# A branch in place of VectorE's bound on a softplus, expert blocks skipped by row count, and a reordered end, in a fused selective-scan, attention and expert kernel

## The chip, the cores and the metric

The kernel runs on one core of a Trainium2 chip. The metric is the device time of one execution in microseconds (us). The engines are called as the profile calls them: PE is TensorE's matmul and PEld its weight load, DVE is VectorE, ACT is ScalarE, POOL is GpSimd, SP is SyncE, which here issues most DMAs. All data are fp32.

## The reference

Four images of 384 channels and 32x32 pixels (L = 1024 tokens) pass two layers.

```
x = x + gelu(LN(cross_merge(selective_scan(cross_scan(group_norm(x))))))   # layer 0
#   four directions k, 16 states n, for each channel d along the 1024 tokens:
#   dt = softplus(w_dt . dts + bias);  h = h*exp(dt*A) + dt*u*B;  y = sum_n h*C
t = tokens(x)
t = t + causal_attention(LN(t))                                            # layer 1
t = t + sum_e gate_e * (gelu(LN(t) w1_e + b1_e) w2_e + b2_e)               # top 2 of 4 experts
```

## The kernel before

**The scan sets the clock.** The layer-0 work is cut into 768 units (4 images, 3 channel blocks, 4 directions, 4 groups of states, 4 groups of channels; 192 units an image). One Python loop of ticks t writes the program; nothing reorders it afterwards, and each engine runs its own instructions in the order in which they were written. In tick t ACT gets the decay of unit t+2 (`decay`, an Exp, tile da), DVE the product `front` (tile v, a PSUM tile, L648) and the scan `middle` (tile h, L654), POOL the product `back` of unit t-1 (h times C, L671), which waits until `front` of tick t is over, and every fourth tick PE gets `row` (L696), 16 matmuls that sum four h tiles into y. There are seven h buffers. In images 1 to 3, `ahead` puts a wait on DVE before `front` in every fourth tick: for the row that was written two ticks earlier. In image 0, 104 units get v from PE instead (L958).

**Beside the scan.** A generator `preparation(b)` makes the inputs of image b while image b-1 is scanned. Its part `project_dt` runs for each direction k and channel block m (48 times; the first two, at the very start, in `first_dt`): PE projects, ACT adds the bias, then the softplus:

```
for x_, log in zip(xs, logs): act(log, x_, AF.Exp)
for log in logs:              act(log, log, AF.Ln, bias=1.0)
nc.vector.scalar_tensor_tensor(x_, log, BOUND, x_, ALU.min, ALU.max)   # L485, BOUND = 80
```

and DVE multiplies by u (L526). Both results go to HBM and come back spread over the partitions.

**Layer 1 behind it.** When an image's scan is over, `finish` (layernorm, gelu, residual), then `behind` (attention, the routing `ready`, the experts) are stepped while the next image is scanned; for the last image they stand alone, which the code calls `alone`. In each tick `go_on` gives such work a budget of PE time: `pace`, 4.4 in attention and 3.1 in the experts; each piece of work says what it costs. The experts of an image take 11 blocks of 256 token rows (NBLK), sorted by expert; block j has twelve parts (six of the first matmul, `first_`, L1591, six of the second, `second_`, L1636) that are charged 2.6 each, and its tokens' transposes 0.9. The order is first(0), first(1), second(0), first(2), second(1), and so on. Weights come by SP in 384 KB pieces (L1497) into eight slots. `by_rows` runs a block with fewer columns, or not at all, from a table of row counts, but only for the last image: PE loads all 11 counts (L1558) and branches (L1561, L1564). There each PSUM bank is first zeroed by DVE (L1584, L1627).

**The end.** `ready` is run for token groups of 4, 2 and 2 blocks of 128: gate scores, softmax over four experts, the comparison that picks two (`cnt`, `sel`), running sums and PE's prefix sums (`place`), the target rows (`places`, L1370), then 16 scatters by POOL (L1385) into the expert order. `combine` gathers each token's two results (POOL, L1682), adds residual, bias and gates on PE (L1708) and writes out (ACT, L1715). For the last image it is split in `early` (first choice, residual, bias) and `late` (second choice).

Of the kernel before, what the change touches and what calls it, by code (L numbers as in the profile page):

```python
# [47 lines left out]
PACE_E = 3.1  # L48
BT = 256
BOUND = 80.0  # L50
# [5 lines left out]
def hybrid_kernel(  # L56
# [419 lines left out]
    def softplus(xs, logs):  # L476

        for x_, log in zip(xs, logs):
            act(log, x_, AF.Exp)
        for log in logs:  # L480
            act(log, log, AF.Ln, bias=1.0)

    def bounded(x_, log):

        nc.vector.scalar_tensor_tensor(x_, log, BOUND, x_, ALU.min, ALU.max)  # L485

    def project_dt(b, pair, m, u, xd):

        both = PAIRS[pair]
        groups = (both,) if b == 0 else ((both[0],), (both[1],))  # L490
        v = u[m]
        for n, ks in enumerate(groups):
            need = 2 * len(ks) + (pair if n == 0 else 0)
            slots.kept = need
            while not slots.ready(need):
                yield "wait", 1
            slots.kept = 0
            if pair == 1 and n == 0:
                v = slots.now(f"ut_{b}_{m}", P, L)
                nc.scalar.copy(v.rearrange("p (w h) -> p w h", h=HW), columns(u[m]))  # L500
            dts = [slots.now(f"dt_{b}_{k}_{m}", P, L) for k in ks]
            dus = [slots.now(f"du_{b}_{k}_{m}", P, L) for k in ks]
            for h in range(NH):
                while not banks.ready(len(ks)):
                    yield "wait", 1
                pss = [banks.now(f"pdt_{b}_{k}_{m}_{h}") for k in ks]
                for i, k in enumerate(ks):
                    o = 64 * pair + 32 * both.index(k)
                    r = slice(o, o + R)
                    nc.tensor.matmul(  # L510
                        pss[i], wdt[r, m * P : (m + 1) * P], xd[r, bass.ts(h, 512)],
                        start=True, stop=True,
                    )
                if h == 0 or clock[0] >= IMAGE:

                    yield "wait", 1
                for i, k in enumerate(ks):
                    act(
                        dts[i][:, bass.ts(h, 512)], pss[i], AF.Identity, bias=dtb[:, k, m : m + 1]
                    )  # L520
                    banks.give(f"pdt_{b}_{k}_{m}_{h}")
            softplus(dts, dus)
            yield "wait", 2
            for i, k in enumerate(ks):
                bounded(dts[i], dus[i])
                nc.vector.tensor_mul(dus[i], dts[i], v)  # L526
                yield "wait", 1
                nc.sync.dma_start(dts_d[b, k][0, m * P : (m + 1) * P, :], dts[i])
                nc.sync.dma_start(dts_d[b, k][1, m * P : (m + 1) * P, :], dus[i])
                if b == 0:  # L530
                    stored_du.add((k, m))
                slots.give(f"dt_{b}_{k}_{m}", f"du_{b}_{k}_{m}")
        if pair == 1:
            slots.give(f"ut_{b}_{m}")
# [4 lines left out]
    def first_dt(u, xd):  # L539
# [13 lines left out]
        softplus(dts, dus)  # L553
        for i, k in enumerate(ks):
            bounded(dts[i], dus[i])
# [664 lines left out]
    def ready(b, h, yb, rows, moments):  # L1220
# [59 lines left out]
        def over(v):  # L1280
# [3 lines left out]
        nc.vector.tensor_reduce(red, sc, AX.X, ALU.max)  # L1284
        nc.vector.tensor_tensor(sc, sc, over(red), ALU.subtract)
        act(sc, sc, AF.Exp)

        cmp = [
            one.tile([P, 4, E, E], F32, tag=f"cmp{i}", name=f"cmp{i}_{name}")[:, :n] for i in range(2)
        ]  # L1290
        each = sc.unsqueeze(3).to_broadcast([P, n, E, E])
        other = sc.unsqueeze(2).to_broadcast([P, n, E, E])
        yield "wait", 1
        nc.vector.tensor_reduce(red, sc, AX.X, ALU.add)
        nc.vector.reciprocal(red, red)
        nc.vector.tensor_tensor(sc, sc, over(red), ALU.mult)
        nc.vector.tensor_tensor(cmp[0], other, each, ALU.is_gt)
        nc.vector.tensor_tensor(cmp[1], other, each, ALU.is_ge)
        nc.vector.tensor_tensor(
            cmp[1], cmp[1], lower.unsqueeze(1).to_broadcast([P, n, E, E]), ALU.mult  # L1300
        )
        nc.vector.tensor_tensor(cmp[0], cmp[0], cmp[1], ALU.max)
        cnt = small("cnt", name, n, E)
        nc.vector.tensor_reduce(cnt, cmp[0], AX.X, ALU.add)

        sel = small("sel", name, E, n)
        nc.vector.tensor_single_scalar(sel.rearrange("p e q -> p q e"), cnt, 1.5, ALU.is_lt)
        cum = counts[b, h] = sm.tile([P, E, n], F32, tag=f"cum{h}", name=f"cum_{name}")
        nc.vector.tensor_tensor_scan(
            cum.rearrange("p e q -> p (e q)"), fresh[n].rearrange("p e q -> p (e q)"),  # L1310
            sel.rearrange("p e q -> p (e q)"), 0.0, op0=ALU.mult, op1=ALU.add,
        )
# [22 lines left out]
        if h == LAST:  # L1335
            for i in range(LAST + 1):
                nc.tensor.matmul(
                    pp[:, 4 * E : 5 * E], ones, last_of(i, False),
                    start=(i == 0), stop=(i == LAST),
                )  # L1340
        yield "pe", 1.5
        mk = small("mk", name, n, E)
        nc.vector.scalar_tensor_tensor(mk, cnt, 1.5, sc, ALU.is_lt, ALU.mult)
        nc.vector.tensor_reduce(red, mk, AX.X, ALU.add)
        nc.vector.tensor_scalar_add(red, red, 1e-9)
        nc.vector.reciprocal(red, red)
        nc.vector.tensor_tensor(mk, mk, over(red), ALU.mult)
# [25 lines left out]
        banks.give(f"place_{name}")  # L1373
        pm = yield from banks.take(f"pm_{name}")
# [7 lines left out]
        placed = places[b]  # L1382
        for q in range(n):
            for i in range(2):
                nc.gpsimd.indirect_dma_start(  # L1385
                    out=views[2 * (q0 + q) + i],
                    out_offset=bass.IndirectOffsetOnAxis(
                        ap=placed[:, q0 + q, i : i + 1], axis=0
                    ),
                    in_=rows[:, q, :], in_offset=None,  # L1390
                )
            if not alone and q < n - 1:
                yield "wait", 1
        routed.add((b, h))
# [16 lines left out]
    def table(b, total):  # L1411
# [6 lines left out]
        nc.vector.tensor_reduce(n, full, AX.X, ALU.add)  # L1418
        up_to = one.tile([1, E - 1, E], F32, tag="up_to", name=f"up_to_{b}")
# [38 lines left out]
    def experts(b, route):  # L1458
# [11 lines left out]
        def look_up(j):  # L1470
            if j not in expert:
# [79 lines left out]
        def by_rows(j, run):  # L1551

            if not alone:
                run(BT)
                return
            if not filled:
                for n in range(NBLK):
                    filled[n] = nc.tensor.value_load(  # L1558
                        tables[b][0:1, 2, n : n + 1], min_val=0, max_val=BT
                    )  # L1560
            with tc.If(filled[j] > P) as whole:  # L1561
                run(BT)
            with whole.Else():
                with tc.If(filled[j] > 0):  # L1564
                    run(P)

        STEP = 3 if alone else 1

        def first_(j):
# [4 lines left out]
            for f0 in range(0, NF, 2 * STEP):  # L1574
# [3 lines left out]
                for f in range(f0, f0 + 2 * STEP, 2):  # L1578
# [4 lines left out]
                    if alone:  # L1583
                        nc.vector.memset(ps, 0.0)  # L1584
# [11 lines left out]
                by_rows(j, run)  # L1596
# [12 lines left out]
                yield "pe", 2.6 * STEP  # L1609
# [8 lines left out]
        def second_(j, gone):  # L1618
            pss = {}
            for c0 in range(0, 6, STEP):  # L1620
                for c in range(c0, c0 + STEP):
                    yield from need(("2", j, c))
                if c0 == 0:
                    for i in range(2):
                        pss[i] = yield from banks.take(f"py_{b}_{j}_{i}")
                        if alone:
                            nc.vector.memset(pss[i][:, :C], 0.0)  # L1627
# [14 lines left out]
                by_rows(j, run)  # L1642
                slots.give(*[tiles["2", j, c][1] for c in range(c0, c0 + STEP)])
                yield "pe", 2.6 * STEP
            yt = yield from slots.take(f"yt_{b}_{j}", P, 2, C)

            def out_():
                for i in range(2):
                    if alone and i == 1:
# [6 lines left out]
                if alone and j == NBLK - 2:  # L1656
                    side.append(early(b))
# [4 lines left out]

        while (b, LAST) not in routed:
            yield "wait", 1
        yield from load(0)
        yield "wait", 1
        yield from turn_(0)
        gone = {}
        for w, j in order_:
            if w == "1":  # L1670
                if j + 1 < NBLK:
                    yield from load(j + 1)
                yield from first_(j)
# [75 lines left out]
    def early(b):  # L1749

        for i in range(L // P):
# [4 lines left out]
            closing[i] = g, z  # L1756
            gather(b, i, g, 0)
            beside(b, i, g, z)
        yield "wait", 3
        for i in range(L // P):  # L1760
            ps = yield from banks.take(f"pz_{b}_{i}")
            add_up(ps, *closing[i], ("t2", "b2", 0), True, False)
            closing[i] = *closing[i], ps
            yield "pe", 2.0

    def late(b):

        for i in range(L // P):
            gather(b, i, closing[i][0], 1)
        for i in range(L // P):  # L1770
            while len(closing[i]) < 3:
                yield "wait", 1
            g, z, ps = closing[i]
            add_up(ps, g, z, (1,), False, True)
            put_out(b, i, ps, z)
# [61 lines left out]
    def go_on():  # L1837
        spare[0] = min(spare[0] + pace[0], pace[0])
# [115 lines left out]
```

## Time and profile before

| | |
|---|---|
| Time, median of 3 runs | 3740.76 us (3736.13 to 3742.01) |
| The profiled execution | 3738.39 us, span 3736.7 us (1.7 us lie around the span) |
| PE, DVE, ACT, POOL busy | 80%, 81%, 55%, 53% |
| First and last scan (L654) start at | 48.9 and 3155.7 us |
| Last row of y written by PE | about 3164 us |
| First query projection of the last image (L1068) | 3228.42 us |
| First expert matmul of the last image (L1591) | 3377.11 us |
| Last real block copied out (L1652); last output copied (L1715) | 3688.56; 3733.03 us |

All durations and places are of the one profiled execution. A row of the groups reads: line, engine, operation, out<-in, count, then busy us, mean ns of one, and the idle time in front of it with what ended it. In the matmul groups one written fp32 matmul is two records.

### The profile page before, as it was taken

To read this page: it belongs to the slowest core of one execution; us is meant where nothing else is said; L and a number is where in the kernel's file an instruction comes from. 1 tells how busy PE (TensorE), PEld (TensorE's weight loads), DVE (VectorE), ACT (ScalarE), POOL (GpSimd) and SP (SyncE) were. 2 spreads that over 40 slices of the span, in tenths; PEclk is the share of its full clock that TensorE was granted. 3 is DMA by queue.
4 is the path that set the end of the run, shared out by engine and by line. 5 is a ranking of instruction groups with operands and counts; after the bars stand their busy time and mean duration, and the time that the engine had idled before them with its cause. 6 is when DMAs were issued, how large, how long until landed. Compare 5 with 4: busy or idle time off the path is not lost. (4 is left out here: it accounts for less than half of the span.)

```text
span 3736.7 us, 41646 instructions
## 1 busy us (share of the span) xinstructions
PE 2996.1 (80%) x13267; PEld 1798.4 (48%) x13267; DVE 3020.3 (81%) x2417; ACT 2061.5 (55%) x3268; POOL 1980.5 (53%) x931
## 2 busy tenths in 40 slices
PE   4566755678589899779569999779589999778997
PEld 1233423334346566344345665344256665556775
DVE  6999888899989999998999999999989998131110
ACT  5778787556466566456546665356356564342121
POOL 2677667645656555764656555765666666010001
PEclk7677777779789999769779999879689999888998
DMA  6658644543577888554567888553378876215555
GB/s 198 216 201 291 241 179 186 201 166 135 195 243 277 293 300 297 198 196 153 177 224 277 292 286 292 193 206 129 123 253 301 294 279 207 76 47 180 180 187 178
DMA packets 405202, 798.42 MB, mean 214 GB/s; under 512 B 47500, under 2 KB 278620, under 8 KB 404972
## 3 DMA queue, kind: packets, MB, share of 16 engines
q1 hardware_dynamic: 390572, 770.01, 59.3%
q0 software_dynamic: 8192, 25.17, 2.1%
q8 instruction: 117, 1.92, 0.2%
q10 hardware_dynamic: 6208, 0.39, 0.1%
q14 instruction: 113, 0.93, 0.1%
HBM read 680.44 MB, written 115.02 MB: 213 GB/s over the span
## 5 line engine op out<-in xcount | busy, mean ns | idle before, releaser
L671 POOL TENSOR_TENSOR h<-h,bc 128x1024 f32<-128x1024 f32 x768 | 1818.4, 2372 | 1208.9 <-DVE v L648 1031.8
L654 DVE TENSOR_TENSOR_SCAN h<-da,v 128x1024 f32<-128x1024 f32 x768 | 1749.3, 2283 | 80.7 <-PE v L958 40.8
L192 ACT ACTIVATE da<-dt,a 128x1024 f32<-128x1024 f32 x768 | 884.7, 1162 | 774.8 <-DVE h L654 636.7
L648 DVE TENSOR_TENSOR v<-du,bc 128x1024 f32<-128x1024 f32 x664 | 851.4, 1282 | 95.9 <-PE y L696 26.2
L696 PE MATMUL y<-h,sel 128*32 128x512 f32 x3072 | 560.0, 703 | 186.2 <-POOL h L671 178.6
L1591 PE MATMUL ph<-turned,w 128*128 128x256 f32 (+1 forms) x2772 | 631.1, 384 | 45.4 <-DMA w<-in_w 32.2
L1636 PE MATMUL py<-w,ht 128*128 128x384 f32 x1776 | 606.2, 493 | 11.3 <-DMA w<-in_w 11.3
L1591 PEld LDWEIGHTS ph<-turned,w 128*128 128x128 f32 x2772 | 523.4, 193 | 164.2 <-issue 51.1
L1636 PEld LDWEIGHTS py<-w,ht 128*128 128x128 f32 x1776 | 335.2, 192 | 277.7 <-issue 40.0
L192 ACT ACTIVATE ht<-ph,b1t 128x256 f32<-128x256 f32 x470 | 196.7, 471 | 330.6 <-PE ph L1591 329.8
L696 PEld LDWEIGHTS y<-h,sel 128*32 128x32 f32 x3072 | 104.4, 120 | 507.7 <-POOL h L671 290.6
L1682 POOL DMA_INDIRECT g<-ysd,places x64 | 83.4, 1303 | 369.6 <-DMA g<-gtd 329.8
L958 PE MATMUL v<-ident,st 128*128 128x128 f32 x832 | 156.5, 351 | 117.4 <-DVE h L654 113.0
L192 ACT ACTIVATE st<-turn,bt 128x128 f32<-128x128 f32 x832 | 245.4, 564 | 0.1
L958 PEld LDWEIGHTS v<-ident,st 128*128 128x128 f32 x832 | 127.7, 183 | 164.0 <-DVE h L654 94.6
L182 ACT ACT_TABLE_LOAD x122 | 156.5, 1283 | 12.2 <-issue 10.1
L510 PE MATMUL pdt<-xd,wdt 12*128 12x512 f32 x184 | 117.2, 774 | 23.5 <-ACT st L192 7.2
L1385 POOL DMA_INDIRECT xsd<-fx,places x32 | 36.3, 1135 | 153.6 <-DVE places L1370 145.8
L1169 PE MATMUL po<-vt,pt 128*128 128x384 f32 x242 | 91.6, 528 | 9.0 <-ACT pt L1059 9.0
L1098 PE MATMUL ss<-axn,qt 128*128 128x512 f32 (+3 forms) x252 | 91.8, 508 | 5.6 <-ACT pr L192 4.5
L192 ACT ACTIVATE dt<-pdt,dtb 128x512 f32<-128x512 f32 x96 | 64.6, 690 | 49.4 <-PE pdt L510 48.1
L192 ACT ACTIVATE ht<-ht 128x3072 f32<-128x3072 f32 x33 | 91.3, 2766 | 0.4
(381 smaller groups left out, 2656.1 us busy)
## 6 DMA issues: line engine op xcount, KB each, us to landing
w<-in_w SPq DMA_DIRECT2D x528, 384.0 KB
bc<-rows SPq DMA_DIRECT2D x384, 512.0 KB
dt<-dts SPq DMA_DIRECT2D x192, 512.0 KB
du<-dts SPq DMA_DIRECT2D x192, 512.0 KB
dts<-dt SPq DMA_DIRECT2D x48, 512.0 KB
dts<-du SPq DMA_DIRECT2D x48, 512.0 KB
xg<-xsd SPq DMA_DIRECT2D x44, 384.0 KB
ysd<-yt SPq DMA_DIRECT2D x44, 384.0 KB
```

The costliest lines, as they stand in the source:

```text
L182: nc.scalar.preload_act_table_set(kind)
L192: return nc.scalar.activation(dst, src, f, **more)
L510: nc.tensor.matmul(pss[i], wdt[r, m * P : (m + 1) * P], xd[r, bass.ts(h, 512)], start=True, stop=True,)
L648: return nc.vector.tensor_tensor(u["v"], spread["du4", n], spread["bc", n][:, 0, :], ALU.mult)
L654: nc.vector.tensor_tensor_scan(u["h"][:, ::step], u["da"][:, ::step], u["v"][:, ::step], 0.0, op0=ALU.mult, op1=ALU.add,)
L671: product = units[n]["product"] = nc.gpsimd.tensor_tensor(h, h, spread["bc", n][:, 1, :], ALU.mult)
L696: units[n]["row"] = nc.tensor.matmul(y, sel, h, start=first, stop=last, tile_position=(0, jj * DJ))
L958: nc.tensor.transpose(u["v"][:, t * P : (t + 1) * P], st[:, t, u["j"] * P : (u["j"] + 1) * P], ident)
L1098: nc.tensor.matmul(ps[:, : e - o], qt[:, c, i * P : (i + 1) * P], xn[o // 512][:, c, : e - o], start=(c == 0), stop=(c == M - 1 and (alone ...
L1169: nc.tensor.matmul(po[:, :C], pts[i][:, j, :], vt[:, j, :], start=False, stop=(j == i))
L1591: nc.tensor.matmul(ps[:, i * BT : i * BT + n], t[:, c, i * P : (i + 1) * P], xt[:, c, :n], start=(c == 0), stop=(c == M - 1),)
L1636: nc.tensor.matmul(pss[i][:, :C], hts[j][:, 2 * c + f, i * P : (i + 1) * P], tiles["2", j, c][0][:, f, :], start=(c == 0 and f == 0), stop ...
```

## The change

1. The softplus. Exp now also gives the sum over its row; PE adds the 128 sums, DVE compares the total with 1e19, POOL and ACT load the answer into a register and branch. The usual way has only the Ln; the other way (POOL and ACT) bounds the argument at 40. DVE's pass L485 is gone from `project_dt`; `first_dt` clips before Exp and takes a maximum after it.
2. `by_rows` holds for all images: PE loads one row count per block in images 0 to 2, branches at each part, and where rows are left out fills the rest of the PSUM bank with transposes. DVE's zeroing is gone. A part is charged 2.2 instead of 2.6.
3. Block 0 is taken as expert 0, so its weights need no table; in the last image four pieces of weights are asked for before the routing is over, and the counts are loaded ahead of the first transposes.
4. Last image: `ready` picks on the raw scores, does the softmax after PE's prefix sums, and scatters before the gates are normalised. Pace is 1.5 after the scan.
5. Last image: residual, gates and bias are fetched from block 2 on (`beside_all`), DVE adds the first choice to the residual (`first_choice`), PE sums up in `late`.

```diff
+PACE_T = 1.5
+PART = 2.2
-BOUND = 80.0
+LIMIT = 1.0e19
+EDGE = 40.0
...
+        sums = sm.tile([P, 2], F32, tag="sums", name=f"sums_{names[0]}")
+        for i, (x_, log) in enumerate(zip(xs, logs)):
+            act(log, x_, AF.Exp, accum_out=sums[:, i : i + 1])
+        return sums
+    def within(sums, n, name):
+        ps = yield from banks.take(f"sums_{name}")
+        nc.tensor.matmul(ps[:1, :n], ones[:, :1], sums[:, :n], start=True, stop=True)
+        yield "wait", 1
+        fits = sm.tile([1, 2], I32, tag="fits", name=f"fits_{name}")
+        nc.vector.tensor_single_scalar(fits[:, :n], ps[:1, :n], LIMIT, ALU.is_le)
+        banks.give(f"sums_{name}")
+        yield "wait", 1
+        return fits
+    def bounded(x_, log, fits):
+        tables_for(LOGS)
+        fit = nc.values_load(
+            fits, engines=[mybir.EngineType.Pool, mybir.EngineType.Activation],
+            min_val=0, max_val=1,
+        )
+        with tc.If(fit != 0) as fast:
             act(log, log, AF.Ln, bias=1.0)
-        nc.vector.scalar_tensor_tensor(x_, log, BOUND, x_, ALU.min, ALU.max)
+        with fast.Else():
+            nc.gpsimd.tensor_scalar_min(log, x_, EDGE)
+            act(log, log, AF.Exp)
+            act(log, log, AF.Ln, bias=1.0)
+            nc.gpsimd.tensor_scalar(x_, x_, -EDGE, 0.0, ALU.add, ALU.max)
+            nc.gpsimd.tensor_tensor(log, log, x_, ALU.add)
...
-            yield "wait", 2
+            yield "wait", 1
+            fits = yield from within(sums, len(ks), f"{b}_{ks[0]}_{m}")
             for i, k in enumerate(ks):
-                bounded(dts[i], dus[i])
-                nc.vector.tensor_mul(dus[i], dts[i], v)
+                bounded(dts[i], dus[i], fits[:, i : i + 1])
+            yield "wait", 1
+            for i, k in enumerate(ks):
+                nc.vector.tensor_mul(dts[i], dus[i], v)
...
-            if not alone:
-                run(BT)
-                return
...
             with tc.If(filled[j] > P) as whole:
                 run(BT)
             with whole.Else():
-                with tc.If(filled[j] > 0):
+                fill(P)
+                with tc.If(filled[j] > 0) as some:
                     run(P)
+                with some.Else():
+                    fill(0)
...
-                    if alone:
-                        nc.vector.memset(ps, 0.0)
...
+                def fill(o):
+                    for f, t, w, name, ps in parts:
+                        for i in range(2):
+                            nc.tensor.transpose(
+                                ps[:, i * BT + o : i * BT + o + P], ident, ident
+                            )
...
-                yield "pe", 2.6 * STEP
+                yield "pe", PART * STEP
...
+        while alone and fetched[0] < 4:
+            while not slots.ready():
+                yield "wait", 1
+            weights()
         while (b, LAST) not in routed:
             yield "wait", 1
         yield from load(0)
+        for j in range(NBLK if alone else 1):
+            count_rows(j)
...
+    def first_choice(b):
+        for i in range(L // P):
+            gather(b, i, closing[b, i][0], 0)
+        yield "wait", 2
+        for i in range(L // P):
+            add_choice(b, i, 0)
+            yield "wait", 0
     def late(b):
         for i in range(L // P):
-            gather(b, i, closing[i][0], 1)
+            gather(b, i, closing[b, i][0], 1)
+        pss = {}
         for i in range(L // P):
-            while len(closing[i]) < 3:
-                yield "wait", 1
-            g, z, ps = closing[i]
-            add_up(ps, g, z, (1,), False, True)
-            put_out(b, i, ps, z)
+            pss[i] = yield from banks.take(f"pz_{b}_{i}")
+            sum_up(b, i, pss[i], False)
...
     def go_on():
+        if clock[0] >= NU + 4:
+            pace[0] = PACE_T
```

## The prediction

> **What bounds the kernel now.** The page's slices first: DVE is full through the scan and nearly idle after it, and PE fills up once in each image. So there are two stages, a scan bounded by DVE and an end bounded by chains and PE.
>
> ```profile
> PE   4566755678589899779569999779589999778997
> DVE  6999888899989999998999999999989998131110
> ```
>
> The timeline inside the scan gives the rhythm. A tick is one L648 and one L654, 1.26 + 2.29 us with small gaps: 3.61 us from L648 to L648. POOL's product begins when L648 ends, is over near the end of the scan, and POOL then idles 1.26 us.
>
> ```profile
> 3143.49 1.25 DVE L648 TENSOR_TENSOR v<-du,bc 128x1024 f32<-128x1024 f32 x1
> 3144.78 2.29 DVE L654 TENSOR_TENSOR_SCAN h<-da,v 128x1024 f32<-128x1024 f32 x1
> 3144.91 2.36 POOL L671 TENSOR_TENSOR h<-h,bc 128x1024 f32<-128x1024 f32 x1 [1.26 <-DVE v L648]
> 3147.10 1.26 DVE L648 TENSOR_TENSOR v<-du,bc 128x1024 f32<-128x1024 f32 x1
> ```
>
> The groups by shape give what DVE does on top, and the sizes of the expert matmuls:
>
> ```profile
> L485 DVE SCALAR_TENSOR_TENSOR dt<-du,dt 128x1024 f32<-128x1024 f32 x48 | 64.1, 1335 | 11.2 <-ACT du L192 11.0
> ...
> L1591 PE MATMUL ph<-turned,w 128*128 128x256 f32 x2724 | 625.0, 386 | 45.4 <-DMA w<-in_w 32.2 <-issue 6.7 <-ACT ht L192 2.9
> L1636 PE MATMUL py<-w,ht 128*128 128x384 f32 x1776 | 606.2, 493 | 11.3 <-DMA w<-in_w 11.3
> ```
>
> Last the windows and the waits. A window's row has its length, then PE, PEld, DVE, ACT and POOL busy, PE's clock, the DMA share and GB/s: in image 2's expert stretch PE and DVE are both full.
>
> ```profile
> 3000.00:3100.00 100.00, 99.07 (x438) 62.81 (x437) 98.09 (x56) 61.47 (x75) 65.29 (x28) 1.00 0.78 275
> ```
>
> A row of the waits has us in total, times and the longest. DVE waited for a row of y 26.2 us in the whole run: PE just keeps up.
>
> ```profile
> DVE v L648 <- PE y L696: 26.2, 14, 6.3
> ```
>
> [...]
>
> **The change part by part.**
>
> *Softplus on DVE.* 46 of the 48 L485 go: 46 x 1.335 = 61.4 us. Added are 41 compares on DVE (36 for one direction, 5 for two in image 0), taken at 0.22 us from small DVE rows of 0.17 us and a gap: 9 us. The ten of image 0 count to four fifths, since DVE is not full there: **-50 us** (-60 to -40). `first_dt` clips before Exp: no row shows it, one L485 more at most, I take **+1** (0 to 3). ACT's sum read costs 0.2 us (the row of accumulator reads), in its idle time.
>
> *The new waits.* POOL loads and branches between two products. SP's loads of the same kind take 0.28 + 0.155 + 0.02 us, a branch 0.07 to 0.44, a jump and a semaphore about 0.2: 0.7 to 1.1 us against 1.26 us of idle. Queued behind it is the next product, and for that the L648 after. Hidden in images 1 to 3 if so; in image 0 two stand together. I take **+5**; at 2.2 us each, uncovered by 0.94, it is 46 x 0.94 = 43. Below nothing it cannot go: POOL loses no work. PE's sum waits for ACT's Exp of the tick before, the compare for PE one tick later: covered while PE lags by less than a tick.
>
> *Expert blocks at a faster pace.* Running the reference's routing on its inputs gives the rows per expert: 543 519 513 473, 511 514 511 512, 509 462 547 530, 520 497 527 504. Cut in 256s, each image has 8 full blocks (over 128 rows); image 0 has 3 small ones besides, image 1 has 1 small and 2 empty, images 2 and 3 have 2 small and 1 empty. The trace of image 3 agrees (144 narrow L1591 records are two blocks of 72). By starts, 12 records of L1591 take 2.59 us (3406.92 to 3409.51) and 48 of L1636 15.5, so a full block is 72 x 0.216 + 48 x 0.3225 + 0.7 for transposes = 31.7 us of PE. Its ticks fall from (12 x 2.6 + 0.9)/3.1 = 10.35 to (12 x 2.2 + 0.9)/3.1 = 8.8. Rows need 1.92 us per four ticks. Before: PE 31.7 + 5.0 + 1 for projections = 37.7, DVE 10.35 x 3.62 = 37.5 to 39.6: level. After: PE 35.9 to 36.8, DVE 32.1 to 32.9: PE falls behind by 3.9 us per full block. Small blocks, now about 23 us of PE, give back 8.
>
> What is queued behind: the next row of y, for which DVE waits in `ahead`, two ticks after it was written. Two ticks are 7.24 us, less 1.7 to its start and 1.92 of its own: 3.6 us of slack. Image 2 (six full in a row, small, two, small): 6 x 3.9 - 3.6 = 20, then 4. Image 1 (four, small, four): 12 + 12. Image 0 (two, small, ...): 4 x 4.2 = 17. Together 65, of which some 23 are waits for rows that DVE has now: **+42 us**. Bounds: 0, if banks and rows absorb it, and 24 x 3.9 = 94 with no slack. Branches stay hidden: the sequencer reached L1561 at 3414.06 while the array was at the third of that step's 12 us.
>
> *Image 2's experts end earlier* (132 parts, 17 ticks), so its `combine` leaves the end and stands in the scan: 16 gathers of 1.3 us on POOL, **+3** (0 to 20).
>
> **The end.** From the last row (3164) to the first projection (3228.4) are 64 us; this chain's own steps, from the timeline, are 46: y taken over 1.3, means 5.4, subtraction 3.5, squares 3.2, variances 2.3, root with its table 1.75, reciprocal 1.75, spread by PE 3.5, product 3.4, gelu with its table 4.8, residual 1.2; then the attention's norm: a square 1.1, sums 3.0, root with table 2.2, reciprocal 1.75, spread 3.8, first product 1.75. The other 18 are spent behind image 2's output: its PE sums between the steps, ACT's copies (a square waited for a sum that had waited 5.1 us for its load), slots held so that the residual came 3.8 us late. With `combine` gone from there: **-18** (-20 to -8). From the last `places` copy (3358.11) to the first expert matmul are 19 us, of which 6.67 are PE's eleven loads, 0.7 each; these now run while the scatters land and the tokens load, and the weights are there. The softmax, 6 small DVE rows and an Exp with its way to ACT and back (1.4 us in all), leaves the chain, and the eight scatters of the first token group, 1.27 us each, no longer stand in front of the last four, since the slower pace puts that group's work before the last attention block. But that work, some 5 us of PE's gate and prefix matmuls, then delays that block: -6.7 - 1.4 - 4 + 5 = **-7** (-14 to 0), the 4 being taken out of the 5.5 us for which POOL was still busy with scatters after the last `places` (to 3363.9). At the end:
>
> ```profile
> 3688.56 0.48 ACT L1652 COPY yt<-v_end 128x384 f32<-128x384 f32 x1 [19.91 <-PE py L1636]
> ...
> 3729.45 0.48 ACT L1715 COPY z<-pz 128x384 f32<-128x384 f32 x1 [5.24 <-PE pz L1708]
> 3733.03 0.48 ACT L1715 COPY z<-y_end 128x384 f32<-128x384 f32 x1 [3.10 <-PE y_end L1708]
> ```
>
> Two rounds of eight gathers (10 us each) and their landings (about 4 each) stay, since the second round still waits for the last block's store, and that store for the first round's reads. PE's last residuals and biases go from behind the last gather: before, the last two token groups' sums started only when banks came free and end at 3733.0, 11 us after the last gather was issued (3721.87); with eight banks taken ahead, a landing of about 4 is left there: **-7** (-10 to 0). The zeroing against the fills: 0, two small blocks x 1.8 us against one wait of 1.9. The slower pace of 1.5 only interleaves: 0 (-8 to 8).
>
> **Sum.** -50 + 1 + 5 + 42 + 3 - 18 - 7 - 7 = -31 on 3738.4: 3707 us. The profiled run lies 2.4 below the median, inside its spread; I leave that.
>
> **The rivals.** (B) PE absorbs the pace: without the 42, 3665 us. For it: h has seven buffers; against: PE's 99 of 100. (C) **Slower: PE becomes the bound of the expert stretches.** With no slack, 94 instead of 42: 3759 us. It decides once the 24 full blocks cost over 73/24 = 3.0 us each net, 73 being all the other gains; I have 1.75. (D) The branch shows on POOL: +38, 3745 us. (E) The guard fails and the other way is taken: [...] the arguments would have to pass 40, which a projection plus a negative bias hardly does.
>
> **Chances.** Forecast 0.45 (3690 to 3735), B 0.22, C 0.20, D 0.10, E 0.03. A measurement tells 0.2%, 7.5 us, from no change. Faster: 0.42 + 0.22 + 0.03 = 0.67; within: 0.03 + 0.02 + 0.05 = 0.10; slower 0.23. The range 3655 to 3765 leaves out about 0.07 below and 0.11 above.
>
> **What would show it.** Scan starts: the last L654 near 3160 (forecast), 3110 (B), 3215 (C). The wait of L648 for y: 70 us, under 30, over 100. POOL's idle in front of L671 after a branch: 1.3, or over 2 (D). L1068 near 46 to 48 us after the last row. If L696 is on time and the scan still ends late, the cost is in POOL or ACT and my PE sum is wrong.

## The result, and the profile after

The kernel after takes **3770.4 us** (median of 4 runs, 3769.93 to 3772.33) against 3741.39 us before (median of 4 as well): ratio 1.0081, 95% interval 1.0064 to 1.0099. It is slower by 29 us; the forecast was 3707 us, and the range ended at 3765. Of the rivals, C (slower, PE as the bound of the expert stretches, 3759 us) went the right way and came closest.

The last scan starts at 3216.1 us instead of 3155.7, which is rival C's sign (3215). Behind the scan the kernel is faster: from the last row of y to the end it takes 543.9 us instead of 572.7. So the profiled span, 3768.5 instead of 3736.7, is **+60.5 in the scan and -28.8 in the end**.

Four views of the profile after. First its slices, in tenths of 40 equal parts: DVE's row is no longer a row of nines up to the end of the scan.

```profile
PE   4766666788599897687599976688499977788998
DVE  6898898989987899989987889989988899330000
```

The window of 100 us inside image 2's expert stretch (length, PE, PEld, DVE, ACT and POOL busy, PE's clock, DMA share, GB/s) says it in one line: PE 100.0 of 100 us, DVE 86.6. Before, both were full (99.1 and 98.1). It is the window in which PE is fullest; the two behind it have PE at 96.7 and 90.8 and DVE at 91.0 and 85.8.

```profile
2750.00:2850.00 100.00, 100.00 (x438) 65.83 (x438) 86.56 (x49) 58.97 (x74) 56.66 (x24) 1.00 0.80 282
```

The timeline at the start of that window shows one such hole. DVE's scan ended at 2745.10; the next L682 stands for 4.99 us until PE gets to the row of y, and POOL's product, which waits for L682, stands for 6.19 us.

```profile
2742.81 2.29 DVE L688 TENSOR_TENSOR_SCAN h<-da,v 128x1024 f32<-128x1024 f32 x1
...
2750.08 1.23 DVE L682 TENSOR_TENSOR v<-du,bc 128x1024 f32<-128x1024 f32 x1 [4.99 <-PE y L730]
2751.35 2.29 DVE L688 TENSOR_TENSOR_SCAN h<-da,v 128x1024 f32<-128x1024 f32 x1
2751.49 2.36 POOL L705 TENSOR_TENSOR h<-h,bc 128x1024 f32<-128x1024 f32 x1 [6.19 <-DVE v L682]
```

The waits (us in all, times, longest): the rows of y cost DVE 87.0 us in place of 26.2, but they are not alone. Loads of dt and du come later (44.0 in place of 25.5), and so does PE's sum for the new compare (12.3, new).

```profile
DVE v L682 <- PE y L730: 87.0, 33, 7.1
DVE v L682 <- DMA du<-dts: 44.0, 23, 5.6
...
DVE fits L492 <- PE sums L489: 12.3, 9, 3.5
```

Adding up DVE's records from the first scan's start to the last's gives the account that the rest of this document uses. It is worked out from the trace of each kernel; "other" is all of DVE's work besides the scan and its product.

| kernel | length | scans | products (L682) | other | idle |
|---|---|---|---|---|---|
| before | 3106.8 | 1750.9 | 850.2 | 346.4 | 207.1 |
| after | 3167.4 | 1751.0 | 872.9 | 278.7 | 314.5 |
| difference | +60.6 | 0 | +22.7 | -67.7 | +107.4 |

DVE was in fact relieved of 68 us. It lost 107 to idling and 23 to products that became longer.

### The profile page after: what moved, and what is told of

It is laid out like the page before. It is cut to its first block, busy times and chain, and to the rows that moved or that the text cites. A ratio compares the mean times of both kernels' runs of the same rounds, so it can differ in the third digit from the quotient of the medians.

```text
span 3768.5 us, 42350 instructions
## 1 busy us (share of the span) xinstructions
PE 2941.6 (78%) x13029; PEld 1712.1 (45%) x13029; DVE 2939.0 (78%) x2338; ACT 2058.8 (55%) x3307; POOL 1991.4 (53%) x931
## 5 line engine op out<-in xcount | busy, mean ns | idle before, releaser
L682 DVE TENSOR_TENSOR v<-du,bc 128x1024 f32<-128x1024 f32 x665 | 874.2, 1315 | 186.7 <-PE y L730 87.0
L730 PE MATMUL y<-h,sel 128*32 128x512 f32 x3072 | 642.6, 726 | 246.6 <-POOL h L705 228.1
L1656 PE MATMUL ph<-turned,w 128*128 128x256 f32 (+1 forms) x2520 | 534.5, 368 | 45.3 <-DMA w<-in_w 40.3
L1706 PE MATMUL py<-w,ht 128*128 128x384 f32 x1440 | 500.4, 494 | 32.3 <-DMA w<-in_w 27.0
L1656 PEld LDWEIGHTS ph<-turned,w 128*128 128x128 f32 x2520 | 450.8, 196 | 126.8 <-issue 29.5
L730 PEld LDWEIGHTS y<-h,sel 128*32 128x32 f32 x3072 | 112.4, 122 | 635.6 <-POOL h L705 387.1
L1706 PEld LDWEIGHTS py<-w,ht 128*128 128x128 f32 x1440 | 270.3, 191 | 241.7 <-issue 49.4
L1767 POOL DMA_INDIRECT g<-ysd,places x64 | 100.6, 1572 | 351.4 <-DMA ysd<-yt 336.9
```

The source lines that it names most:

```text
L682: return nc.vector.tensor_tensor(u["v"], spread["du4", n], spread["bc", n][:, 0, :], ALU.mult)
L730: units[n]["row"] = nc.tensor.matmul(y, sel, h, start=first, stop=last, tile_position=(0, jj * DJ))
L1656: nc.tensor.matmul(ps[:, i * BT : i * BT + n], t[:, c, i * P : (i + 1) * P], xt[:, c, :n], start=(c == 0), stop=(c == M - 1),)
L1706: nc.tensor.matmul(pss[i][:, :C], hts[j][:, 2 * c + f, i * P : (i + 1) * P], tiles["2", j, c][0][:, f, :], start=(c == 0 and f == 0), stop ...
L1767: nc.gpsimd.indirect_dma_start(out=g[:, k * C : (k + 1) * C], out_offset=None, in_=ys_d[0], in_offset=bass.IndirectOffsetOnAxis(ap=places[ ...
```

## The experiments

All are edits of the kernel after. Times are medians, with the ratio to the kernel before on the same chip. The runs stand on several chips, on which the kernel before took 3742 to 3745 us. What is read inside a run, as the start of its last scan, comes from one profiled execution; executions of one kernel differ by several us (oldsoft26: 3731.1 to 3744.7), so that differences of a few us are not resolved.

### The pace of the expert parts: 2.4, and 2.6 as before

```diff
-PART = 2.2
+PART = 2.4            # run part24
...
-PART = 2.2            # run part26, with
-PACE_A = 4.4
+PART = 2.6
+PACE_A = 5.2
```

> The kernel after, with a part charged 2.4 instead of 2.2: a block takes 9.6 ticks instead of 8.8, about 2.8 us more of DVE time. Theory 1 (the pace: PE lags DVE by some 4 us in each full block, DVE waits for rows of y, 87 us in all after against 26 before, and the gathers of combine fall into ticks that have nothing else for DVE): the wait for y falls to about 45 us, and the time to about 3725. Theory 2 (the new softplus eats its own gain in waits, the pace is harmless): 3770, unchanged.

> The kernel after, with a part charged 2.6 as before; the attention's pace goes from 4.4 to 5.2, since attention would otherwise still hold the buffer of one image when the next needs it. Theory 1 (pace): the wait for y is back near 26 us in the expert stretches, combine of image 2 is back behind the scan (some 15 us at the end), time about 3700. Theory 2 (softplus): about 3770, or above by what the faster attention costs.

part24: **3720.66 us**, 0.9943 (0.9926 to 0.9959). part26: 3725.2 us, 0.9958 (0.9942 to 0.9974). One constant, 2.2 to 2.4, turns the loss of 29 us into a gain of 21. In part24 the last scan starts at 3136.0, 80 us earlier than after; DVE's idle falls from 314.5 to 249.4, the wait for y from 87.0 to 59.7, and the products from 872.9 to 857.1. Theory 2 (the softplus eats its own gain) is out. The new softplus does not go with the old pace while the attention's pace is unchanged (last section); with that at 5.2, units 576 to 672, which hold attention, take 450.9 us where part24 takes 434.7, and the gain of the slower experts is spent there. That is why part26 missed its 3700.

### The old softplus under three paces

```diff
-            sums = softplus(dts, dus, [f"{b}_{k}_{m}" for k in ks])
-            yield "wait", 1
-            fits = yield from within(sums, len(ks), f"{b}_{ks[0]}_{m}")
+            softplus(dts, dus)        # Exp, Ln, and DVE's pass, as before
+            yield "wait", 2
...
 PART = 2.2     # oldsoft; 2.4 in oldsoft24, 2.6 in oldsoft26
```

> The kernel after, with the softplus of before (DVE's pass back, no sum, no branch), everything else as after, part at 2.2. Theory 1 (pace): the softplus is worth its 50 to 68 us of DVE time, less what PE's lag hides, as the expert stretches wait for PE anyway: 3800 to 3825. Theory 2 (the softplus's waits eat its gain): 3770 or below.

> The kernel after, with the softplus of before and a part charged 2.6 as before: what is left of the change is the skipping in images 0 to 2 and the new end. Theory 1 (pace): 3741 less about 14 at the end (routing, last combine) and a few us of waits for y that the small and empty blocks save: 3715 to 3730. Theory 2: the same, since it has neither; a value above 3745 would put the loss into the skipping itself (branches, fills), a third theory.

> The kernel after with the softplus of before, a part charged 2.4: the partner of the run with 2.4 (3720.7). At 2.2 the new softplus was worth 41 us of its 68 us of DVE time, since PE's lag covered the rest. At 2.4, with less lag, it should be worth more: 45 to 60, so 3766 to 3780. If it is worth 41 whatever the pace, 3762; if its gain depended on the faster pace, under 3750.

oldsoft: **3811.76 us**, 1.0192 (1.0175 to 1.0209). oldsoft24: 3752.37 us, 1.0017 (1.0009 to 1.0025). oldsoft26: 3736.55 us, 0.9985 (0.9973 to 0.9997).

| run | last scan starts | products | other | idle | last row to end |
|---|---|---|---|---|---|
| oldsoft26 | 3156.8 | 850.9 | 346.7 | 207.6 | 571.4 |
| oldsoft24 | 3194.9 | 870.6 | 343.9 | 229.5 | 538.9 |
| oldsoft | 3254.8 | 872.8 | 343.3 | 289.1 | 544.2 |
| after | 3216.1 | 872.9 | 278.7 | 314.5 | 543.9 |

These pairs take the change apart. *Before to oldsoft26* is the skipping of rows in images 0 to 2 and the new end at the old pace: the scan ends 1.1 us later, DVE idles the same, and the new end is worth 1.3 us (571.4 for 572.7). So its time missed the 3715 to 3730 that I expected. *oldsoft26 to oldsoft* is the pace alone: the scan ends **98.0 us** later, 81.5 of it more idle time, 21.9 longer products. *oldsoft to after* is the softplus alone: DVE's other work falls by 64.6 us, 25.4 of which come back as idle time, and the scan ends **38.7 us** earlier. In the scan the new softplus is worth 58.8 us at 2.4 (3194.9 to 3136.0). As whole times, oldsoft24 and part24 differ by only 32 us, under the 45 that I expected: with the old softplus the gathers of image 2's `combine` start at unit 752, in the scan, with the new one at unit 766, so that it stands behind the scan, which costs 37 us there (538.9 against 575.8). Why it comes later is not shown.

### Half of PE's expert work left out

```diff
-            with tc.If(filled[j] > P) as whole:
+            with tc.If(filled[j] > BT) as whole:
```

> The kernel after, but every expert block runs on its first 128 rows only and fills the rest: half of the expert matmuls are left out, the program, its ticks and DVE's work stay. Read in the scan alone. Theory 1 (DVE waits because PE's throughput falls short in full blocks): L682's waits for y fall from 87 to under 30 us and the last scan starts at 3216 less 50 to 75, 3140 to 3165; the lengthened L682 beside the gathers (some 2 us each, ticks of 4.3 us) stays. Theory 3 (it is the order of the instructions at the faster pace, banks or branches, not the amount of PE work): the last scan stays above 3190.

Half of the experts' rows are left out, so this is not the function any more; only the scan is read, in the single execution of this run. The last scan starts at **3095.9 us**, 120 earlier than after and well below what I expected. The windows of this run, for 100 us of the same expert stretch:

```profile
2750.00:2850.00 100.00, 79.88 (x492) 52.58 (x492) 98.10 (x56) 67.21 (x91) 64.83 (x28) 0.98 0.87 306
```

PE is at 79.9 and DVE back at 98.1. The waits of this run:

```profile
DVE v L682 <- DMA du<-dts: 28.8, 16, 5.8
DVE v L682 <- PE y L730: 28.4, 11, 5.8
...
DVE fits L492 <- PE sums L489: 3.5, 4, 1.3
```

With the same program, ticks and branches, DVE's idle falls by 118.8 us (314.5 to 195.7). Only 58.6 of that are rows of y; dt and du loads give back 15.2, the compare 8.8, and the rest many small waits. The transfers are the same, at a DMA share of 0.87 in place of 0.80, so they do not hold the scan back. It is the amount of PE work in a tick, and it reaches DVE by more ways than the row. The products stay long (873.8), so those have another cause.

### Where the longer products come from

The timeline of after, in image 2's last ticks, while `combine` gathers:

```profile
3122.19 2.35 POOL L705 TENSOR_TENSOR h<-h,bc 128x1024 f32<-128x1024 f32 x1
3123.65 1.99 DVE L682 TENSOR_TENSOR v<-du,bc 128x1024 f32<-128x1024 f32 x1
...
3124.70 1.81 POOL L1767 DMA_INDIRECT g<-ysd,places  x1 [0.16 <-issue]
...
3125.67 2.29 DVE L688 TENSOR_TENSOR_SCAN h<-da,v 128x1024 f32<-128x1024 f32 x1
...
3126.53 2.35 POOL L705 TENSOR_TENSOR h<-h,bc 128x1024 f32<-128x1024 f32 x1
3127.99 1.99 DVE L682 TENSOR_TENSOR v<-du,bc 128x1024 f32<-128x1024 f32 x1
```

These are bare ticks: DVE has the scan and its product alone. Here POOL is the one that never rests: 2.35 for the product, 1.81 for the gather, 0.18 between, a tick of 4.34 us instead of 3.62. L682 begins while the product has 0.89 us to go, takes 1.99 instead of 1.26, and ends 1.10 us behind the product.

It is so in both traces. In after, 412 L682 begin under a product of POOL that has 0.90 us or less to go, and each ends 1.09 to 1.22 us behind it; in before, 458 L648 end 1.09 to 1.23 us behind it. Those with nothing of POOL's beside them, 236 and 187, take 1.20 to 1.24 us. A front that began with 0.82 us or more of the product to go took 1.9 us and more. What holds DVE up is not shown.

The traces tie these fronts to the gathers. Fronts of 1.9 us and more number 15 in before, 16 in oldsoft26, 48 in after and 49 in oldsoft; 45 of the 48 begin within 6 us of a gather's start, and three images have 48 gathers.

> The kernel after (parts at 2.2), with image 2's combine held back until the last image's finish is over, so that its 16 gathers leave the bare ticks at the end of the scan and stand beside the last image's attention, where POOL has nothing to do. Theory 1 on gathers (each lengthens its tick by 0.7 us): last scan near 3205 instead of 3216, from the last row to the first projection still about 38, attention up to 3 us longer; 3757 to 3763. Theory 2 (gathers beside the scan cost nothing, as in the prediction's +3): 3770.

> The same with a part charged 2.4: in the run with 2.4 alone (3720.7) the combine of image 2 stood behind the last row and the first projection came 72 us after it. If it is combine that fills these 34 us over the 38 of the kernel after, the gap falls to 38 to 42 and the time to about 3688. If the finish chain is held by something else that runs late at 2.4, 3715 to 3720.

```diff
     def combine(b):
-        yield "wait", 2
+        while b == B - 2 and b + 1 not in finished:
+            yield "wait", 1
```

late22: 3854.86 us, 1.0304 (1.028 to 1.0327). late24: 3777.1 us, 1.0083 (1.0064 to 1.0102). The scan side held: in units 672 to 767 the products fall from 132.0 to 120.8 us and the stretch from 379.8 to 368.4, 11 us for a `combine` with its 16 gathers. (The last scan starts only 5.9 us earlier, at 3210.2; the stretches ahead of `combine` took some 5 us more in this execution.) The end did not: the first projection comes 126 us (late24: 127) after the last row, against 37.5. The timeline of late22 shows why. The eight blocks of `combine` now go one behind the other, 12 us each, every one waiting some 6 us for the load of its tokens, and the attention norm's sums (L1034) stand behind the last of them in PE's queue.

```profile
3289.38 1.62 PE L1793 MATMUL pz<-ident,z 128*128 128x128 f32 x6 [6.01 <-DMA z<-t2d]
...
3301.21 1.62 PE L1793 MATMUL pz<-ident,z 128*128 128x128 f32 x6 [5.78 <-DMA z<-t2d]
...
3331.54 2.19 PE L1034 MATMUL y_end<-yb,mean_w 128*32 128x128 f32 x48 [0.57 <-ACT z L1800]
```

I had counted POOL's idleness there and forgotten the rest of `combine`: its loads, its slots and its place in PE's order.

### A pace for each image, and the fills

```diff
-PART = 2.2
+PART = (2.4, 2.35, 2.25, 2.2)
...
-                yield "pe", PART * STEP
+                yield "pe", PART[b] * STEP
```

The second run (mix_clear) also has DVE zero the banks of the last image, as before, in place of PE's fills there.

> The kernel after, with a part charged 2.4 in image 0, 2.35 in image 1, 2.25 in image 2 and 2.2 in the last: images 0 and 1 at a pace that PE holds, image 2 just fast enough that its combine is over (tick 769) when the last image's finish starts (tick 771). Theory 1: the two images gain about 50 us of scan against the kernel after, image 2 some 6, and the gap from the last row to the first projection stays at 38 us (72 at 2.4): 3707 to 3717. If the gap does not depend on combine, 3740 or so.

> The same, and in the last image alone DVE zeroes the banks as in the kernel before, instead of PE's 57 fill transposes of 0.29 us (16.5 us of PE). If the fills are what made the last image's expert stretch 7 us longer (318.6 against 311.4 from the first to the last expert matmul), that comes back: 5 to 8 us under the run before, 3700 to 3710; if it was the new work beside it, no difference.

mix: 3722.36 us, 0.9942 (0.993 to 0.9955). mix_clear: 3722.93 us, 0.9946 (0.9934 to 0.9959). Both lie above what I expected (3707 to 3717, and 3700 to 3710 if the fills cost anything). The gap behind the last row is 38.0 us, as expected, and the scan of image 2 pays for it: units 576 to 767 take 820.4 us where part24 takes 793.4, and units 480 to 576 10 us more. So mix is no better than part24; what `combine` costs behind the scan, the faster pace costs in it. The fills make no difference to the time: without them 60 transposes go (8.7 us of PE in mix; I had counted 57 and 16.5 us), and PE waits 7.18 us where DVE zeroes, put down by the profile to a load of weights, as the kernel before waited 7.62. Why the last image's expert stretch is 7 us longer than before (318.6 against 311.4, also 319.1 without fills) stays open; oldsoft26 has it too (318.9).

### The guard

```diff
         tables_for(LOGS)
-        fit = nc.values_load(...)
-        with tc.If(fit != 0) as fast:
-            act(log, log, AF.Ln, bias=1.0)
-        with fast.Else():
-            ...
+        act(log, log, AF.Ln, bias=1.0)   # nobranch24; in noguard24 row sums,
+                                         # PE's sum and the compare go too
```

> The kernel after at 2.4, without the guard: no row sums, no PE sum, no compare, no load and no branch; Exp and Ln stay at the same ticks (the other way, for large arguments, is left out). Against 3720.7: if the guard costs what its visible rows say (41 compares of 0.13 us, 12 us of waits of the compare for its sum), 3700 to 3712; if branches on POOL and ACT cost more that the waits don't show (rival D of the prediction), 3680 or less; if all is covered, 3720.

> The kernel after at 2.4, with the guard's row sums, PE's sum and DVE's compare kept, but no load and no branch behind them (Ln always; the other way, for large arguments, is left out). The run without the guard was 14 us faster than the 3720.7 with all of it. If that is the compare (DVE stands before it until PE's queue reaches the sum), this run stays at 3718 to 3724. If it is the branches of POOL and ACT (rival D), it falls to 3704 to 3709.

noguard24: **3706.46 us**, 0.9896 (0.9873 to 0.9919). nobranch24: 3717.01 us, 0.9923 (0.9902 to 0.9943). Both leave out the way for large arguments. Against part24 the whole guard costs 14 us by the medians and 17 by the start of the last scan. The run without branches alone is 3.7 us faster than part24, inside the intervals, so the branch is not shown to cost anything; nor is the split between branch and compare settled beyond that (the last scans start at 3136.0, 3127.4 and 3118.7). The compare's cost can be seen in after: PE does a row of y and only then the sum, and DVE stands before the compare for 3.49 us with the next product behind it.

```profile
1230.42 1.93 PE L730 MATMUL y<-h,sel 128*32 128x512 f32 x16
...
1232.16 0.19 PE L489 MATMUL sums<-sums,ones 128*1 128x1 f32 x2
...
1232.53 0.15 DVE L492 TENSOR_SCALAR fits<-sums 1x1 int32<-1x1 f32 x1 [3.49 <-PE sums L489]
```

part24, mix and mix_clear are 21 to 23 us faster than before; of those with the whole computation part24 is the simplest.

## Why the prediction was wrong

The account of the forecast, against what the runs show for the same terms (differences of the profiled spans):

| term | predicted | measured | from |
|---|---|---|---|
| softplus with guard, first_dt | -50 + 1 + 5 = -44 | -38.7 | oldsoft to after, scan |
| pace, with image 2's combine | +42 + 3 = +45 | **+98.0** | oldsoft26 to oldsoft, scan |
| skipping rows at the old pace | inside the 42 | +1.1 | before to oldsoft26, scan |
| the end | -18 - 7 - 7 = -32 | -28.8 | before to after |
| sum | -31 | +31.6 | span: +31.8 |

**Softplus: right in kind, near in size by luck, since two errors cancel.** DVE's relief was larger than I said, 64.6 us: the 46 passes were 60.3, the multiplies behind them became 5.4 shorter, and the 41 compares took 0.126 us each, 5.2 in all, not 9; the other 4 are not traced to a part. But 25 us came back as idle time at this pace. "Covered while PE lags by less than a tick" was the right condition; PE lags by more.

**Expert blocks at a faster pace: the mechanism was right, the size wrong, and this is the step that failed.** I priced the block well: in image 2 of after, the transposes in front of successive full blocks start at 2782.27, 2818.11 and 2853.89 us, 35.8 us apart, and my PE time for a block was 35.9 at the least, 3.9 over DVE's. What I then took off was wrong. First the 3.6 us of slack in front of each run of full blocks, then the 23 us of waits "that DVE has now", as if the new waits replaced the old ones. My own upper bound without slack, 24 x 3.9 = 94, less the 23, is 71; the idle measured for the pace alone is 81.5. The wait for y was forecast at 70 and came to 87. The rest came in ways that I had not listed: the run with half of the expert work shows as much idle time given back outside the row's wait (60 us) as in it (59). What else stood in PE's queue was late as well: projections and so the stores and loads of dt and du (15.2 us given back in that run), the sum for the compare (8.8). Rival C decided at "3.0 us each net"; the pace cost 98.0 / 24 = 4.1.

**Image 2's experts end earlier, +3: the mean of a mixed group.** I took 1.3 us for a gather from the page. That is the mean over two kinds. The traces of before and after have them, as minimum, median and maximum in ns:

```profile
L1682 POOL DMA_INDIRECT g<-ysd,places x64: 943/992/1977, 1529.6 to 3720.9; - x64
L1767 POOL DMA_INDIRECT g<-ysd,places x64: 942/1796/1813, 1449.2 to 3754.1; - x64
```

All 47 slow ones of after (1.79 to 1.81 us) began under a product of DVE that had 0.93 to 0.95 us to go, and ended 0.85 to 0.88 us behind it; the other 17 took 0.94 to 1.00. Before's four that began under a scan took 0.99 each; here is one:

```profile
1585.92 2.27 DVE L654 TENSOR_TENSOR_SCAN h<-da,v 128x1024 f32<-128x1024 f32 x1
1586.08 0.99 POOL L1682 DMA_INDIRECT g<-ysd,places  x1 [0.16 <-issue]
```

In the bare ticks the gather came under the product. With 0.16 for its issue it then took 1.97 us of the 1.26 that POOL had, 0.71 us a tick and 11.4 for 16, which is what late22 gave back. And it was not one image: in before, image 0's gathers ran around the start of the next image's attention, in ticks with other work for DVE (units 384 to 480: 443.8 us, 4.6 a tick), and image 1's likewise (units 576 to 672: 425.4 us, 4.4 a tick); at the faster pace nearly all stand in bare ticks. The products grew by 21.9 us in all.

**The end: near in sum, -28.8 for -32, by luck in its parts.** The finish chain gained more, 64.4 to 37.5 us from last row to first projection (-27 for -18). That this is `combine`'s doing, as forecast, the runs bear out: where nearly all its gathers are issued beside the scan, the gap is 37 to 38 us (after, oldsoft, oldsoft24, half, mix, mix_clear), where most come behind it 64 to 73 (before, oldsoft26, part24, part26, and both runs on the guard). So these 27 us belong to the pace too, which cost 98.0 - 27.2 = 71 us in all from oldsoft26 to oldsoft, where I had 45 - 18 = 27. From there to the first expert matmul 148.7 became 142.9 (-5.8 for -7). From the last expert matmul to the end 48.2 became 44.9 (-3.3 for -7), and the expert stretch took back 7.2 that I had at 0. These parts together gave some 2 us, not 14.

**The rivals.** B is refuted: DVE idles 107 us more. D is not seen: POOL's row of the groups has the same 931 instructions, no pass of the other way is among them, and nobranch24 gains nothing clear. E is refuted by the same count. The sign that I set for C, a last scan near 3215, is what came; its second sign, over 100 us of waits for y, did not, since half of the cost stands elsewhere. I gave C 0.20 and took the forecast's slack, an unshown number, for the likelier case.

## What to carry to other kernels

Where one engine was at 99 of 100 in a stage, a faster schedule came back here as idle time of the other engine (81.5 us for the pace alone), and by more than the wait that I had in mind (for y, 87.0 us in after), because other work in the full engine's queue was late as well; take slack off such a price only where the trace shows it. Relief of the other engine (here 65 us of DVE) was worth most where the schedule was tightened less: at 2.4 the scan gained 59 of it, at 2.2 39. Before pricing a group that moves, split its mean by what runs beside it.

## What was unexpected

- A gather issued by POOL took 0.94 to 1.01 us with DVE idle or in a scan (after and before), and 1.8 us where it began under a product of DVE with 0.94 us to go. In a bare tick it lengthened the tick by 0.7 us (4.34 for 3.62), so 16 of them cost 11 us.
- POOL's load of the register and its branch ran in its sequencer while the engine still did the product: in the trace of after, the load starts at 1234.04 and the branch is past at 1234.65, under a product that lasts from 1234.05 to 1236.40. It is so for 37 of the 46 loads; five of the others are second loads of a pair in image 0 and fall between two products. This fits a branch that is not seen to cost anything, with no need of the 1.26 us of idle time that I had set against it.
- Softplus and pace are not independent. With the new softplus, parts at 2.6 and the attention at 4.4 leave one image's attention with a buffer that the next image already needs, so that one of the two paces has to be changed: that is the order in which the program lays out its ticks, not a measurement. With the old softplus 2.6 and 4.4 go together (oldsoft26).
